# Loading the next image into a tile of its own during the last MLP, with its statistics taken there and its chunks copied on GpSimd

## The chip, the core and the metric

The kernel runs on one core of one Trainium2 chip. The metric is the device time in microseconds (us) of one execution; lower is better. The engines of the core run side by side, each with its own queue in order: TensorE (PE, with its weight loads as PEld), VectorE (DVE), ScalarE (ACT), GpSimd (POOL), and SyncE (SP), which here only issues DMAs.

## The reference, cut to what matters

Four images of 56 x 56 pixels and 128 channels pass through four layers. Each layer reads the group norm of its input and adds its result to it. Layers 0 and 3 are the same block with other weights.

```python
def _gn(v, G=32, eps=1e-5):
    B_, H_, W_, C_ = v.shape
    g = v.reshape(B_, H_, W_, G, C_ // G)
    m = jnp.mean(g, axis=(1, 2, 4), keepdims=True)
    s = jnp.var(g, axis=(1, 2, 4), keepdims=True)
    return ((g - m) / jnp.sqrt(s + eps)).reshape(v.shape)

x = x + L0(_gn(x), ...)   # window attention, full attention, MLP
x = x + L1(_gn(x), ...)   # 3x3 convolution, four selective scans (mamba)
x = x + L2(_gn(x), ...)   # deformable convolution
x = x + L3(_gn(x), ...)   # as L0
```

The blocks L0 and L3 ("swin" in the kernel) compute, for an image x:

```python
xs = roll(x, (-3, -3)); wins = 7 x 7 windows of xs
x = roll(windows_back(mha(wins)), (3, 3))
xf = x + mha(layernorm(x))             # attention over all 3136 pixels
xf = xf + gelu(layernorm(xf) @ w1 + b1) @ w2 + b2
```

The statistics of the group norm are over a whole image, so no part of a layer can start before the last pixel of its input is there.

## The kernel before, in words

An image lies on chip as one tile `x` of 128 channels (partitions) by 3136 pixels, float32. `x` is allocated once and holds every image in turn and every layer's result. All layers cut the 3136 columns into seven chunks of 448 (`NCK` chunks of `CH`).

`run` (L1415) loads image 0 into `x` and then, for each of the four images, takes the seven statistics (`stats`, L115: one `bn_stats` on VectorE for each chunk, into the small tile `gn_st`) and calls the layers L0, mamba, deform and L3. Inside a layer the statistics for the next layer are taken as each chunk is stored, so that the loop of `stats` in `run` is needed only where an image comes in.

A swin block is `attention` and then `mlp`. `attention` begins with `group_norm` (L123): the seven statistics are aggregated (L128, VectorE), two products of one column on TensorE average over groups (L130, L137), ScalarE takes a square root (L139) and VectorE its reciprocal (L140). Then come the windows, eight bands of them, in the order 3, 4, 5, 6, 7, 0, 1, 2. `tokens` (L230) zeroes the padded tiles of a band on GpSimd for the first two bands (memsets at L232 and L238; further ones for `ks`, `qs` and `kl` at L336, L337 and L391) and writes the normalized pixels of the band (L235: on VectorE for the first two bands, on GpSimd for the others). The full attention follows. It takes nearly all of a block's time.

`mlp` (L653) works through the chunks in the order 3, 4, 5, 6, 0, 1, 2 (`cols`). For each chunk `residual` adds the attention's result (L667, L668), `center`, `spread`, `scale` and `shift` are the layer norm (L154, L674 on GpSimd, L180, L679, L683, L687), `hidden` and `result` are the two products with the gelu between (L694, L695, L701), and `store` adds the chunk's result and writes it to `x` (L705, VectorE). The order in each queue is written out by hand: the loop at its end calls these steps for different chunks in turn, and a scheduler keeps that order within the block.

After a store, the L0 MLP takes the chunk's statistics. The L3 MLP (`last` is the number of the image there) calls `finish` instead: a DMA on SP writes the chunk to the output, and if there is a next image, a second DMA on SP loads the next image's chunk into the same columns of `x`. It waits until the first has landed. The seven statistics of the new image are issued by `run`, and stand among the MLP's instructions on VectorE as its scheduler placed them.

Of the kernel before, what the change touches and what calls it, by code (L numbers as in the profile page):

```python
# [10 lines left out]
F32 = mybir.dt.float32  # L11
# [8 lines left out]
P = 128  # L20
HW = 56
L = HW * HW
CH = 448
NCK = L // CH
# [54 lines left out]
class _Net:  # L79
# [573 lines left out]
    def mlp(self, layer, x, x1, oT, last):  # L653


        nc, tc, w = self.nc, self.tc, self.w[layer]
        with tc.tile_pool(name="mlp", bufs=2) as sb, tc.tile_pool(name="mlp_ps", bufs=8, space=PSUM) as ps, tc.manual_schedule():
            bank = lambda name: ps.tile([P, 512], F32, tag="mm", name=name)
            x2, m = x1, {}

            def cols(n):
                c = (n + 3) % NCK
                return slice(c * CH, (c + 1) * CH)

            def residual(n):
                py = bank("py2")
                nc.tensor.matmul(py[:, :CH], lhsT=w["wo"], rhs=oT[:, n * CH : (n + 1) * CH], start=True, stop=True)  # L667
                nc.vector.scalar_tensor_tensor(x2[:, cols(n)], py[:, :CH], w["boe"], x1[:, cols(n)], ALU.add, ALU.add)  # L668

            def center(n):  # L670
                (m["pc", n],) = self.ln_center([x2[:, cols(n)]], bank)
                m["sq", n] = sb.tile([P, 2, CH], F32, tag="ln_sq", name="ln_sq")
                nc.scalar.activation(m["sq", n][:, 0, :], m["pc", n][:, :CH], AF.Square)
                nc.gpsimd.tensor_add(x2[:, cols(n)], x2[:, cols(n)], x[:, cols(n)])  # L674

            def spread(n):
                sq = m["sq", n]
                self.ln_root(sq[:, 1, :], sq[:, 0, :], bank)
                nc.vector.reciprocal(sq[:, 1, :], sq[:, 1, :])  # L679

            def scale(n):
                sq = m["sq", n]
                nc.vector.tensor_mul(sq[:, 0, :], m.pop(("pc", n))[:, :CH], sq[:, 1, :])  # L683

            def shift(n):
                m["xn", n] = sb.tile([P, CH], F32, tag="xn2", name="xn2")
                nc.scalar.activation(m["xn", n], m.pop(("sq", n))[:, 0, :], AF.Identity, bias=w["be2"], scale=w["g2"])  # L687

            def hidden(n, fs):
                for f in fs:  # L690
                    if f == 0:
                        m["h", n] = sb.tile([P, 4, CH], F32, tag="h", name="h")
                    ph = bank("ph")
                    nc.tensor.matmul(ph[:, :CH], lhsT=w["w1"][:, f * P : (f + 1) * P], rhs=m["xn", n], start=True, stop=True)  # L694
                    nc.scalar.activation(m["h", n][:, f, :], ph[:, :CH], AF.Gelu, bias=w["b1"][:, f : f + 1])  # L695

            def result(n):
                h = m.pop(("h", n))
                py = bank("py3")
                for f in range(4):  # L700
                    nc.tensor.matmul(py[:, :CH], lhsT=w["w2"][:, f * P : (f + 1) * P], rhs=h[:, f, :], start=(f == 0), stop=(f == 3))  # L701
                m["py", n] = py

            def store(n):
                nc.vector.scalar_tensor_tensor(x[:, cols(n)], m.pop(("py", n))[:, :CH], w["b2"], x2[:, cols(n)], ALU.add, ALU.add)  # L705
                if last is not None:
                    self.finish(last, x, cols(n))
                else:
                    self.stats(x, (n + 3) % NCK)

            def do(f, n, *args):
                if 0 <= n < NCK:
                    f(n, *args)

            residual(0)
            residual(1)
            center(0)
            residual(2)
            spread(0)
            for n in range(-1, NCK):  # L720
                do(hidden, n, (0, 1))
                do(scale, n + 1)
                do(center, n + 2)
                do(hidden, n, (2, 3))
                do(shift, n + 1)
                do(residual, n + 4)
                do(spread, n + 2)
                do(result, n)
                do(store, n)


    def mamba_prepare(self):
# [673 lines left out]
                    product(NCK - 1, i)  # L1406
                add(NCK - 1)

    def finish(self, b, x, cols):

        self.nc.sync.dma_start(self.out[b][:, cols], x[:, cols])
        if b + 1 < self.B:
            self.nc.sync.dma_start(x[:, cols], self.x_in[b + 1][:, cols])

    def run(self):  # L1415
        x = self.x
        self.nc.sync.dma_start(x, self.x_in[0])
        self.swin_prepare("L0")
        self.swin_prepare("L3")
        self.mamba_prepare()  # L1420
        self.deform_prepare()
        for b in range(self.B):
            for c in range(NCK):
                self.stats(x, c)
            self.swin("L0", x)
            self.mamba(b, x)
            self.deform(b, x)
            self.swin("L3", x, last=b)
# [89 lines left out]
```

## Time and profile before

| what | us |
|---|---|
| time, median of 3 runs | 13293.08 (13291.37 to 13294.18) |
| profiled execution, its own time | 13095.61 |
| profiled execution, span from first to last instruction | 13093.7 |
| PE busy | 11654.7 (89% of the span) |
| VectorE busy | 9728.0 (74%) |
| ScalarE busy | 7560.0 (58%) |
| GpSimd busy | 9942.8 (76%) |
| mean granted TensorE clock | 0.943 of full speed |

The profiled execution is one run of its own, and 1.5% shorter than the median of the timed ones. One image takes about 3270 us of the span: the last stores of images 0, 1 and 2 start at 3276.30, 6546.27 and 9812.85 us. Busy shares are averages over stages with different limits; what happens between two images is seen only in the timeline at those places. In a line of the timeline the first number is the start in us from the start of the span, the second the duration in us, then come the engine, the line of the kernel, the operation, the tile written and the tiles read, the shapes, and the count of instructions merged into the line. A bracket gives the engine's idle time ahead of the line and what ended it. Of several instructions merged, the duration is that of all.

### The profile page before, as it was taken

To read this page: it belongs to the slowest core of one execution; us is meant where nothing else is said; L and a number is where in the kernel's file an instruction comes from. 1 tells how busy PE (TensorE), PEld (TensorE's weight loads), DVE (VectorE), ACT (ScalarE), POOL (GpSimd) and SP (SyncE) were. 2 spreads that over 40 slices of the span, in tenths; PEclk is the share of its full clock that TensorE was granted. 3 is DMA by queue.
4 is the path that set the end of the run, shared out by engine and by line. 5 is a ranking of instruction groups with operands and counts; after the bars stand their busy time and mean duration, and the time that the engine had idled before them with its cause. 6 is when DMAs were issued, how large, how long until landed. Compare 5 with 4: busy or idle time off the path is not lost. (4 is left out here: it accounts for less than half of the span.)

```text
span 13093.7 us, 216642 instructions
## 1 busy us (share of the span) xinstructions
PE 11654.7 (89%) x84932; PEld 7362.6 (56%) x84932; DVE 9728.0 (74%) x11883; ACT 7560.0 (58%) x19097; POOL 9942.8 (76%) x6852
## 2 busy tenths in 40 slices
PE   8989996799898999679989899967999989996799
PEld 4438884444543888444454388844445438884444
DVE  6659996665665999666566599966656659996665
ACT  5567772356556777235655677723565567772356
POOL 4949995498494999549759499954974949995497
PEclk9999997899999999789999999978999999997899
DMA  1000003200000000420000000042000000004200
GB/s 59 1 14 4 5 4 114 74 1 9 3 1 14 4 5 4 116 72 1 10 2 1 14 5 5 4 120 68 1 11 1 1 14 5 5 4 121 66 1 6
DMA packets 155644, 317.88 MB, mean 24 GB/s; under 512 B 19660, under 2 KB 89344, under 8 KB 154496
## 3 DMA queue, kind: packets, MB, share of 16 engines
q0 software_dynamic: 80640, 231.28, 6.1%
q1 hardware_dynamic: 73696, 71.21, 1.8%
q8 instruction: 672, 11.01, 0.3%
q14 instruction: 348, 2.85, 0.1%
q10 hardware_dynamic: 288, 1.53, 0.0%
HBM read 256.04 MB, written 47.90 MB: 23 GB/s over the span
## 5 line engine op out<-in xcount | busy, mean ns | idle before, releaser
L569 POOL TENSOR_TENSOR es<-es,e 128x896 f32<-128x896 f32 x2016 | 4159.3, 2090 | 133.1 <-ACT e L563 75.1
L363 DVE TENSOR_REDUCE mx<-pm 128x1 f32<-128x512 f32 (+1 forms) x4928 | 3057.9, 671 | 1401.5 <-PE pm L362 787.3
L563 ACT ACTIVATE e<-pst 128x448 f32<-128x448 f32 (+1 forms) x5600 | 2678.4, 544 | 1886.8 <-PE pst L561 1351.4
L1083 DVE TENSOR_TENSOR_SCAN hs<-da,dbu 128x928 f32<-128x928 f32 x1792 | 3633.1, 2070 | 52.2 <-ACT dbu L1076 30.0
L1092 POOL TENSOR_TENSOR hs<-hs,cb 128x896 f32<-128x896 f32 x1792 | 3473.8, 1951 | 25.0 <-ACT carry L1087 20.3
L362 PE MATMUL pm<-ks,qs 32*128 32x512 f32 (+1 forms) x9856 | 2906.1, 633 | 13.3 <-DVE nm L384 7.8
L561 PE MATMUL pst<-qs,ks 32*128 32x448 f32 x11200 | 2684.0, 547 | 0.0
L1101 PE MATMUL yt<-w_C,hs 128*116 128x128 f32 x14336 | 1865.1, 273 | 1.1 <-POOL hs L1092 1.1
L556 PE MATMUL pst<-nm,sel 32*128 32x448 f32 x5600 | 1637.1, 614 | 0.0
L1101 PEld LDWEIGHTS yt<-w_C,hs 128*116 128x116 f32 x14336 | 1571.2, 135 | 2.1 <-POOL hs L1092 2.1
L1065 PE MATMUL dbu<-dgb,ut 112*128 112x224 f32 x7168 | 1258.6, 298 | 268.0 <-DVE hs L1083 267.8
L585 PE MATMUL po<-e,va 128*32 128x448 f32 (+1 forms) x11200 | 1350.8, 551 | 0.0
L362 PEld LDWEIGHTS pm<-ks,qs 32*128 32x128 f32 x9856 | 923.4, 185 | 746.2 <-DVE mx L363 619.3
L1065 PEld LDWEIGHTS dbu<-dgb,ut 112*128 112x128 f32 x7168 | 946.2, 192 | 533.1 <-DVE hs L1083 523.3
L1265 POOL DMA_INDIRECT g<-tab,idx x1008 | 940.8, 933 | 393.6 <-issue 283.1
L1019 ACT ACTIVATE da<-dl,A 128x112 f32<-128x112 f32 x3584 | 1193.9, 382 | 0.1
L561 PEld LDWEIGHTS pst<-qs,ks 32*128 32x128 f32 x11200 | 1096.8, 185 | 100.9 <-issue 12.7
L556 PEld LDWEIGHTS pst<-nm,sel 32*128 32x128 f32 x5600 | 569.9, 184 | 739.9 <-DVE mx L363 387.1
L1379 PE MATMUL pvt<-w_C,g 112*128 112x112 f32 x2016 | 366.7, 338 | 623.4 <-issue 520.4
L1380 ACT COPY vt<-pvt 128x336 f32<-128x336 f32 x336 | 147.2, 438 | 1126.5 <-PE pvt L1379 1126.5
L288 POOL TENSOR_TENSOR pz<-s,m 64x784 f32<-64x784 f32 x128 | 191.8, 1498 | 751.9 <-DVE m L285 520.0
L1087 ACT COPY carry<-hs 128x32 f32<-128x32 f32 x1792 | 397.2, 222 | 624.0 <-DVE hs L1083 615.9
(237 smaller groups left out, 15945.1 us busy)
## 6 DMA issues: line engine op xcount, KB each, us to landing
g<-tab,idx POOLq DMA_INDIRECT x1008, 3.4
tab<-zero SPq DMA_DIRECT2D x4, 3364.0 KB
dl_d<-dl SPq DMA_DIRECT2D x28, 448.0 KB
dl<-dl_d SPq DMA_DIRECT2D x56, 224.0 KB
tab<-gt SPq DMA_DIRECT2D x16, 448.0 KB
out_dram<-x SPq DMA_DIRECT2D x28, 224.0 KB
tab<-gt SPq DMA_DIRECT2D x16, 336.0 KB
x<-in_x_dram SPq DMA_DIRECT2D x21, 224.0 KB
```

The costliest lines, as they stand in the source:

```text
L362: nc.tensor.matmul(pm[:, :m], lhsT=qs[head(h), q.start : q.start + P], rhs=ks[head(h), keys], start=True, stop=True)
L363: nc.vector.tensor_reduce(mx[:, home[i][1], h, kc : kc + 1], pm[:, :m], AX.X, ALU.max)
L556: nc.tensor.matmul(t[:, :CH], lhsT=self.sel[head(h), :], rhs=nm[head(h), part(qc)], start=True, stop=False)
L561: nc.tensor.matmul(t[:, :CH], lhsT=ks[head(h), k * KB : (k + 1) * KB], rhs=qs[head(h), part(qc)], start=False, stop=True)
L563: nc.scalar.activation(e[:nk, j, :], t[:nk, :CH], AF.Exp, scale=SCALE)
L569: nc.gpsimd.tensor_tensor(s, es[g - 1, p][:nk] if k == 1 else s, e[:nk], ALU.add)
L585: nc.tensor.matmul(m["po"][head(h), :CH], lhsT=va[:nk, k, head(h)], rhs=src(h)[:nk], start=(k == 0), stop=(k == NKB - 1))
L1019: nc.scalar.activation(m["da"][:, :, n, 2:], dl(), AF.Exp, scale=A[:, j, n : n + 1])
L1065: nc.tensor.matmul(pu[:, 8 * h : 8 * h + 8, 2 + tb * TB : 2 + (tb + 1) * TB], lhsT=made[g]["ut", 2 * r + tb][:, d, :], rhs=made["r", g // ...
L1083: nc.vector.tensor_tensor_scan(flat(pairs[u // 2][:, d % 2]), flat(made[g]["da"][:, r]), flat(banks.pop(u)), 0.0, ALU.mult, ALU.add)
L1092: nc.gpsimd.tensor_tensor(hs, hs, made["r", g // 2]["cb"][:, :, r * HW : (r + 1) * HW], ALU.mult)
L1101: nc.tensor.matmul(sums[q][:YR, e * P : (e + 1) * P], lhsT=hs[:, n, :], rhs=self.ident, start=(n == 0), stop=(n == NST // 2 - 1), is_trans ...
```

## The change

In the L3 MLP of every image but the last, a tile `ahead` of a whole image is allocated, and one DMA on SP loads the next image into it at the start of the MLP. After each store the chunk's output DMA is issued as before, and then the statistics of one chunk of `ahead` are taken. One step later in the loop, GpSimd copies that chunk from `ahead` to `x` (`replace`), which has to wait until the output DMA has read the old chunk; the last copy stands behind the loop. `finish` goes, and `run` takes the statistics only for the first image.

```diff
             x2, m = x1, {}
 
+            ahead = None
+            if last is not None and last + 1 < self.B:
+                ahead = sb.tile([P, L], F32, tag="ahead", name="ahead", bufs=1)
+                nc.sync.dma_start(ahead, self.x_in[last + 1])
+
...
             def store(n):
                 nc.vector.scalar_tensor_tensor(x[:, cols(n)], m.pop(("py", n))[:, :CH], w["b2"], x2[:, cols(n)], ALU.add, ALU.add)
                 if last is not None:
-                    self.finish(last, x, cols(n))
-                else:
-                    self.stats(x, (n + 3) % NCK)
+                    nc.sync.dma_start(self.out[last][:, cols(n)], x[:, cols(n)])
+                if last is None or ahead is not None:
+                    self.stats(x if last is None else ahead, (n + 3) % NCK)
+
+            def replace(n):
+                if ahead is not None:
+                    nc.gpsimd.tensor_copy(x[:, cols(n)], ahead[:, cols(n)])
...
                 do(result, n)
                 do(store, n)
+                do(replace, n - 1)
+            replace(NCK - 1)
...
-    def finish(self, b, x, cols):
-
-        self.nc.sync.dma_start(self.out[b][:, cols], x[:, cols])
-        if b + 1 < self.B:
-            self.nc.sync.dma_start(x[:, cols], self.x_in[b + 1][:, cols])
-
...
         for b in range(self.B):
-            for c in range(NCK):
+            for c in range(NCK if b == 0 else 0):
                 self.stats(x, c)
```

## The prediction

> **What bounds the kernel now.** I read the page first. PE is busy for 89% of the span, and PE has the largest share of the chain that ended last; nothing in the page names the step from one image to the next. So I went to the step itself, at 3276 us (image 0 to 1), in the timelines of VectorE (DVE) and GpSimd (POOL). Columns: start, duration, engine, line, what, and in brackets the idle time before and what ended it.
>
> ```profile
> 3275.45 0.63 DVE L117 BATCH_NORM_STATS2 gn_st<-x 128x6 f32<-128x448 f32 x1 [3.19 <-DMA x<-in_x_dram]
> 3276.30 0.68 DVE L705 SCALAR_TENSOR_TENSOR x<-py,w_L,x 128x448 f32<-128x448 f32 x1 [0.23 <-PE py L701]
> 3281.52 0.63 DVE L117 BATCH_NORM_STATS2 gn_st<-x 128x6 f32<-128x448 f32 x1 [4.54 <-DMA x<-in_x_dram]
> 3282.18 0.34 DVE L128 BATCH_NORM_AGGREGATE gn_mv<-gn_st 128x2 f32<-128x42 f32 x1
> ...
> 3286.25 0.16 DVE L140 RECIPROCAL gn_rstd<-gn_rstd 128x1 f32<-128x1 f32 x1 [2.31 <-ACT gn_rstd L139]
> 3286.53 0.89 DVE L235 TENSOR_SCALAR xw<-x,gn_mean,gn_rstd 128x343 f32<-128x343 f32 x3
> ```
>
> The last store of the image starts at 3276.30. Its chunk goes out (issued 3277.01), the next image's chunk is loaded over it (issued 3278.99, when the output has landed), and only then do the last statistics run, at 3281.52. From the last store to the aggregate it is 5.88 us here, 5.80 at the second step (6546.27 to 6552.07) and 5.84 at the third (9812.85 to 9818.69): a wait for DMA on an idle machine. The chain of work that ended last, in order of time, agrees for the third step:
>
> ```profile
> 9815.53 2.48 DMA x<-in_x_dram
> ```
>
> So the transfer is on the path, three times per run, for under 6 us each.
>
> The same piece of code without a load exists in this trace, where the L0 MLP is followed by the mamba stage:
>
> ```profile
> 859.80 0.68 DVE L705 SCALAR_TENSOR_TENSOR x<-py,w_L,x 128x448 f32<-128x448 f32 x1 [4.67 <-PE py L701]
> 860.52 0.63 DVE L117 BATCH_NORM_STATS2 gn_st<-x 128x6 f32<-128x448 f32 x1
> 861.25 0.34 DVE L128 BATCH_NORM_AGGREGATE gn_mv<-gn_st 128x2 f32<-128x42 f32 x1
> ...
> 864.85 0.16 DVE L140 RECIPROCAL gn_rstd<-gn_rstd 128x1 f32<-128x1 f32 x1 [2.11 <-ACT gn_rstd L139]
> ```
>
> Here the aggregate follows the last store by 1.45 us, and the reciprocal follows the aggregate by 3.60 us; at the image step that is 4.07.
>
> What GpSimd does meanwhile matters for the change. At each image step it zeroes the tiles of the next attention in one train of eleven memsets, 3276.26 to 3285.21, and the first normalization (L235 on VectorE) starts at 3286.53, after the train. At the other attention, L3, no load is waited for and the two meet. In image 3:
>
> ```profile
> 12242.82 1.81 POOL L238 MEMSET pz<- 128x2048 f32 x1
> 12244.57 0.53 POOL L232 MEMSET xw<- 128x512 f32 x1
> 12245.03 0.74 POOL L238 MEMSET qp<- 128x768 f32 x1
> 12245.72 1.41 POOL L238 MEMSET kb<- 128x1568 f32 x1
> 12247.06 1.81 POOL L238 MEMSET pz<- 128x2048 f32 x1
> ```
> ```profile
> 12243.86 5.63 DVE L235 TENSOR_SCALAR xw<-x,gn_mean,gn_rstd 128x343 f32<-128x343 f32 x3
> ```
>
> Three instructions that take 0.89 us take 5.63, and end just behind the last memset (12248.87). In images 0, 1 and 2 (2437.20, 5707.60, 8973.90) the same three take 1.46, 1.10 and 1.36: they waited for the memset that was running and got in before the next. So VectorE was let in 3 times of 4, once at the same offset within the train as the time it was not.
>
> [...] here, issued by SP, the output takes 1.98 us from its issue to the issue that waits for it. [...] the trace of before has no GpSimd copy. [...] granted clock 1.00 up to 3280 us, 0.50 from 3281 to 3290.
>
> **The change, part by part** (image step at 3276; times of before unless "new").
>
> Load: 21 loads of 224 KB become 3 of 1568 KB, one at the start of each last MLP but the final one. SP has nothing else queued there. The tile takes over memory of the attention, which ends between 3208 (last scores) and 3215 (last GpSimd multiply L611, 3213.79 to 3214.93). The first image's load, of the same size, was issued at 2.12 and read at 16.01, with the weights in the same queues: 13.9 us at most. New landing 3229 at the latest; the first reader follows the first store at 3234.26. Slack over 5 us, cost nothing. If that cover were gone, VectorE would stand at its head with the MLP's next scale (L683) behind it, and the delay would count nearly in full.
>
> Statistics: 21 in number before and after. Now each stands behind its store and ahead of the next L683. The L0 MLP has just that order, and runs from its first L668 to its last store in 62.74 us (797.06 to 859.80); the L3 MLP before also takes 62.74 (3213.56 to 3276.30). PE is the bound there, and the 0.55 us hide. Nothing.
>
> SP: the waits of the loads on the outputs vanish; they held only SP.
>
> Copies on GpSimd: 21 new ones. Bounds for one: a memset of 512 takes 0.52, the two-input L674 of the same shape 1.13[...]. I take 0.6. Copies 0 to 4 fall in gaps of 6 to 8 us between L674s; copy 5 waits for its output (issued 3271.00) and is done by 3274. None of these is on a path: their cover is GpSimd's 16.13 us of idle time before the memsets. Copy 6 waits for the last output: 3279.0, ends 3279.6. The memsets are queued behind it on GpSimd, since their tiles reuse the MLP's memory; their train moves from 3276.26 to 3279.55, +3.3 us.
>
> Path: new aggregate 3276.30 + 1.45 = 3277.75 (gain 4.43). New reciprocal +3.60 = 3281.35: the PE's two tiny products now come before the clock drops, 0.47 gained. L235 is ready 0.28 later, at 3281.63, against 3286.53: **4.90 us earlier**, if nothing is in its way. But the train of memsets is: "kb" runs from 3279.55+1.57 = 3281.12 to 3282.52. If VectorE gets in behind it, L235 starts at 3282.52, and the gain is **4.0 us**. If it does not, it waits for the train's end, 3279.55+8.95 = 3288.50, and the step is 2.0 us *longer* than before. Copy 6 may also hold L134/L135 ([...]new 3278.83 to 3279.24) for up to 0.6; the wait for "kb" absorbs that. With a copy of 1.13 the train starts at 3280.1, L235 meets "qp" and starts at 3281.7 (gain 4.8), or at 3289.0 (loss 2.5). Later users of the zeroed tiles have room: the second tokens' tile is zeroed by new 3284.7 and wanted near 3288.
>
> Nothing else moves: first image, other stages and the final tail (no load there) are as before. Sum: 3 x 4.0 = 12.0 us. The profiled execution took 13095.61 us (span 13093.7); it would take 13083.6. The median of the runs shown is 13293.08, 1.5% more than the profiled execution, and I take the gain over unscaled, since it is made of DMA and VectorE time: **13281**.
>
> **Rivals.**
> 1. *The lock is lost at every step* (ends slower). Place: L235 against the memset train on GpSimd, which copy 6 has pushed into its way. Price: 2.0 to 2.5 lost at each step instead of 4.0 gained: +6 to +7.5, 13299 to 13301. It decides if VectorE loses at more than two steps of three. For it: image 3 of L3. Against: 3 of 4 meetings went the other way. Chance 0.08.
> 2. *Mixed*: one or two steps lost, gain 6.0 or 0: 13287 to 13293. Chance 0.33.
> 3. *No meeting*: the memsets are issued ahead of copy 6, or miss L235: up to 3 x 4.9 = 14.7, 13278. Chance 0.08.
> 4. *The load comes late*, so that the tile does not do what it is for: some 5 us of VectorE standing per step, +3 to +15 in the sum. Against: the slack above. Chance 0.03.
> Forecast 0.45; 0.03 for something I don't see.
>
> **How the numbers follow.** One measurement of this kernel can tell about 0.2%, 26.6 us, from no change. Every case above is inside that. Range: rival 3 less the 2.8 us spread of the runs shown and some margin, 13273, to nearly all steps lost, 13298; that leaves out rivals 1, 4 and the unseen, 0.14. Faster by over 0.2% would need twice what the wait holds: 0.03. Slower 0.03. Within 0.94.
>
> **What would show it.** Right: L117 in the L3 MLPs with no DMA wait; L128 1.45 us behind the last L705; the "ks" memset 3 us later, behind a copy; L235 stretched to near 1.5 us (won) or over 6 us (lost). Wrong: an L117 waiting for the load, an L705 that comes later than before, copies longer than 1.2 us, or a gain beyond 4.9 us at a step.

## The result, and the profile after

| | before, us | changed, us | ratio (95% interval) |
|---|---|---|---|
| timed together, medians of 13 runs each | 13296.54 | 13290.79 (13278.94 to 13302.19) | 0.9995 (0.9987 to 1.0003) |
| timed again later (18 and 13 runs) | 13110.45 | 13101.2 | 0.9992 (0.9984 to 1.0) |

No difference that a measurement of this kernel can tell. The forecast was 13281, range 13273 to 13298; the median lies 10 us above the forecast.

The profiled execution of the changed kernel took 13278.94 us (span 13277.0), against 13095.61 of before. The two spans must not be subtracted. From L2's `gn_rstd` to L3's of the same image, through the deform stage, in which nothing was changed, it is 395 to 399 us in this trace, 351 in that of before, and 351 to 354 in a second trace of the changed kernel; over four images that is 180 of the 183 us by which the two spans differ. So everything below is measured inside the image step, from the start S of the last store.

The timeline of VectorE and GpSimd of the changed kernel at the first image step (start, duration, engine, line, what; in brackets the idle time before and what ended it):

```profile
3330.34 0.68 DVE L710 SCALAR_TENSOR_TENSOR x<-py,w_L,x 128x448 f32<-128x448 f32 x1 [4.79 <-PE py L706]
3330.95 0.62 DVE L117 BATCH_NORM_STATS2 gn_st<-ahead 128x6 f32<-128x448 f32 x1
3331.60 0.34 DVE L128 BATCH_NORM_AGGREGATE gn_mv<-gn_st 128x2 f32<-128x42 f32 x1
...
3333.07 0.56 POOL L718 COPY x<-ahead 128x448 f32<-128x448 f32 x1 [5.44 <-DMA out_dram<-x]
...
3334.59 0.74 POOL L238 MEMSET qp<- 128x768 f32 x1
...
3335.26 0.16 DVE L140 RECIPROCAL gn_rstd<-gn_rstd 128x1 f32<-128x1 f32 x1 [2.11 <-ACT gn_rstd L139]
3335.27 1.41 POOL L238 MEMSET kb<- 128x1568 f32 x1
3335.53 3.10 DVE L235 TENSOR_SCALAR xw<-x,gn_mean,gn_rstd 128x343 f32<-128x343 f32 x3
3336.61 1.97 POOL L238 MEMSET pz<- 128x2048 f32 x1
3338.53 0.57 POOL L232 MEMSET xw<- 128x512 f32 x1
```

The wait for the load is gone: L117 follows the store, L128 stands 1.26 us behind it (before 5.88), the reciprocal 4.92 (9.95). But the copy has pushed the memsets, and L235, which took 0.89 us behind the finished train, takes 3.10 in the middle of it. The groups of that stretch, shapes kept apart (busy us, mean ns, idle before):

```profile
L235 DVE TENSOR_SCALAR xw<-x,gn_mean,gn_rstd 128x28 f32<-128x28 f32 x1 | 1.8, 1807 | 0.0
L235 DVE TENSOR_SCALAR xw<-x,gn_mean,gn_rstd 128x21 f32<-128x21 f32 x1 | 1.6, 1626 | 0.0
L235 DVE TENSOR_SCALAR xw<-x,gn_mean,gn_rstd 128x343 f32<-128x343 f32 x1 | 1.4, 1354 | 0.1
```

(The recorded durations of queued pieces overlap, so they add to more than 3.10.) A piece of 28 elements per partition took longer (1.81 us) than one of 343 (1.35). The first piece waited for "kb" and was let in: it ended at 3336.88, 0.20 behind the end of "kb" (3336.68). Then "pz" got in, and the small pieces waited for the whole of it: they ended at 3338.61 and 3338.63, "pz" at 3338.58; "pz" is itself 1.97 long instead of 1.81. In the chain of work that ended last, at the third step, L235 now stands where the transfer of 2.48 us stood before:

```profile
9971.30 0.17 DVE gn_rstd L140
...
9971.92 2.81 DVE xw L235 x3
9974.73 0.14 issue
9974.86 1.64 PE pq L243 x2
```

The rest is as it was: from its first L673 (before's L668) to its last store the MLP takes 62.74 us, before and after, with PE busy for 58.96 of it both times; its load is issued at 3262.40 and first read at 3288.80, without a wait.

The three steps, us behind the start of the last store (step 1, 2, 3):

| | before | changed | changed, second trace |
|---|---|---|---|
| reciprocal L140 | 9.95, 9.87, 9.91 | 4.92, 4.91, 4.92 | 4.92, 4.91, 4.92 |
| end of the three L235 | 11.12, 11.03, 11.43 | 8.29, 8.28, 8.33 | 8.29, 8.29, 8.32 |
| first softmax reciprocal L285 | 22.85, 22.75, 23.16 | 20.04, 21.82, 21.81 | 21.79, 21.82, 21.85 |

So 5 us are won at L140, 2.8 are left behind L235, and at most steps 1 is left at the first softmax. The second loss is TensorE's clock. Busy time of each engine by stretch of the changed kernel's trace, in the order PE, PE's weight loads, VectorE, ScalarE, GpSimd (with the count of instructions), then the granted clock, the DMA share and GB/s; first the first step, then the second:

```profile
3334.80:3338.20 3.40, 0.00 (x0) 0.00 (x0) 2.83 (x4) 3.33 (x6) 3.40 (x3) 0.50 0.00 0
3338.20:3341.60 3.40, 2.81 (x5) 1.56 (x6) 0.43 (x2) 0.80 (x3) 3.40 (x5) 0.50 0.00 0
3341.70:3345.00 3.30, 1.58 (x13) 1.42 (x12) 1.81 (x4) 3.05 (x7) 3.30 (x4) 1.00 0.01 2
```

```profile
6656.00:6659.30 3.30, 2.30 (x4) 1.38 (x5) 0.84 (x2) 1.02 (x4) 3.30 (x5) 0.50 0.00 0
6659.40:6662.70 3.30, 2.39 (x10) 1.81 (x10) 1.01 (x3) 2.65 (x7) 2.62 (x2) 0.50 0.00 0
6662.80:6666.10 3.30, 3.30 (x11) 3.30 (x12) 1.13 (x3) 1.36 (x2) 1.44 (x3) 0.50 0.00 0
6666.30:6669.00 2.70, 2.70 (x16) 2.13 (x15) 1.55 (x3) 0.52 (x1) 0.00 (x0) 1.00 0.00 0
```

The clock falls to 0.50 some 4 us behind S and comes back 6.83 us later at step 1, 13.65 at step 2, and 10.24 in the kernel before: two, four and three times 3.41. At step 1 the first stretch of that length with work on PE is 83% busy (2.81 of 3.40), and the clock is back at its end, 11.3 behind S. At step 2 the clock fell half a microsecond earlier (at S+4.0 instead of 4.45); the same work fills 70% of its stretch (2.30 of 3.30), the next holds a wait and fills 72% (2.39 of 3.30), the one after it is filled (3.30 of 3.30), and the clock is back only at 17.65. That the busy share of a stretch decides is the author's estimate from these stretches: no run varied it alone, and later in the trace a stretch of 3.41 us with PE busy throughout (from 3519.12) was followed by another at 0.50. The first products of the attention then run at half clock (0.50), and the first softmax comes 13.5 us behind L235's end instead of 11.75.

### The profile page after: what moved, and what is told of

It reads as the page before. It is cut to its first block, busy times and chain, and to the rows that moved or that the text cites. A ratio compares the mean times of both kernels' runs of the same rounds, so it can differ in the third digit from the quotient of the medians.

```text
span 13277.0 us, 216663 instructions
## 1 busy us (share of the span) xinstructions
PE 11557.6 (87%) x84932; PEld 7332.0 (55%) x84932; DVE 9744.4 (73%) x11883; ACT 7557.7 (57%) x19097; POOL 9960.9 (75%) x6873
## 4 chain that ended last, share of the span: by engine, by line
PE 61%; DVE 19%; another core or an unknown queue 6%; ACT 6%; issue 4%; POOL 3%; DMA 0%; SPq 0%; ACTq 0%; DVEq 0%; POOLq 0%
PE pm L362 13%; DVE hs L1094 12%; PE po L585 9%; PE pst L561 6%; PE pst L556 4%; PE yt L1112 4%; PE dbu L1076 4%; PE pyb L1128 2%; POOL hs L1103 2%; DVE mx L363 2%; DVE dgb L980 2%; PE pvt L1390 2%; PE pd L574 2%; PE pss L270 1%
## 5 line engine op out<-in xcount | busy, mean ns | idle before, releaser
L561 PEld LDWEIGHTS pst<-qs,ks 32*128 32x128 f32 x11200 | 1098.4, 185 | 102.1 <-issue 13.7
L1390 PE MATMUL pvt<-w_C,g 112*128 112x112 f32 x2016 | 333.4, 332 | 905.9 <-issue 563.5
L1390 PEld LDWEIGHTS pvt<-w_C,g 112*128 112x128 f32 x2016 | 283.9, 184 | 984.1 <-issue 646.9
```

The costliest lines, as they stand in the source:

```text
L561: nc.tensor.matmul(t[:, :CH], lhsT=ks[head(h), k * KB : (k + 1) * KB], rhs=qs[head(h), part(qc)], start=False, stop=True)
```

## The experiments

The theory: the 2.2 us by which L235 is stretched (3.10 instead of 0.89) are waits for memsets that GpSimd is running, met piece by piece and not once for the group, and where the copy has put the train of memsets decides what L235 meets. (The recorded texts call this wait the lock; the word stands for the measured wait and for nothing behind it.) The rival: L235 waits for data or for GpSimd's count, or the copy itself holds it. Two more questions: whether the long L3 starts come from the program (an L3 start is the three L235 at the beginning of L3's attention, "blocked" where they take over 5 us; "draw" is used for a meeting whose outcome is not foreseen), and where the rest of the step could go. e0, e1, e3, e7 and e10 are one run each, and 18 runs of the kernel before spread over 46 us (13088.27 to 13133.97), so these five are read by their traces and not by their times.

**e0_before_again: the kernel before once more.** No edit.

> The kernel before, unchanged, for a second trace of it beside the other runs. Nothing is removed. [...]at the three image steps the three L235 follow the train of memsets and take 0.9 us, ending 11.1 us behind the last store; at the four L3 starts each of them is a draw, 1.1 to 1.5 us (let in) or near 5.6 us (blocked to the train's end), and the pattern need not be that of the first trace (in, in, in, blocked). Rival, a fixed order of events: the same pattern as in the first trace, 1.46, 1.10, 1.36 and 5.63 us. Total: if the 198 us by which the profiled executions of before and of the changed kernel differ come from the execution, this one may lie anywhere from 13096 to 13300.

Measured: 13104.4 us. Image steps 11.03, 11.04 and 11.44, as before; L3 starts 1.23, 1.10, 1.36 and 1.25 us: none blocked. Not a fixed order of events.

**e1_one_port: L235 in another form.**

```diff
-                (nc.vector if t < 2 else nc.gpsimd).tensor_scalar(xv[:, a, r, c], self.piece(img, at), gn[0], gn[1], ALU.subtract, ALU.mult)
+                src = self.piece(img, at)
+                if t < 2:
+                    for k in range(a.stop - a.start):
+                        dst = xv[:, a.start + k, r, c]
+                        nc.vector.scalar_tensor_tensor(dst, src[:, k], gn[0], gn[1][:, :, None].to_broadcast(list(dst.shape)), ALU.subtract, ALU.mult)
+                else:
+                    nc.gpsimd.tensor_scalar(xv[:, a, r, c], src, gn[0], gn[1], ALU.subtract, ALU.mult)
```

> The changed kernel with L235 for the first two tokens made one scalar_tensor_tensor per window (9 instead of 3 instructions for the first token; the second operand is rstd spread over the window)[...]. The train of memsets stays where it is. Theory [...]: nine pieces of 0.12 to 0.17 us run beside the memsets, first start 5.2 us behind the last store, last end 6.4 to 6.8 us behind it, where the changed kernel has 8.3; and at all four L3 starts the group takes under 2 us, so about 5 us at the image steps and 4 to 13 us at L3 are saved in the whole run. Rival (L235 waits for data or for GpSimd's count[...]): the last end stays at 8.3 us or later, and one or more of the L3 starts still take over 5 us.

Measured: 13101.75 us (one run; before beside it 13107.7). Its timeline at the first step:

```profile
3292.41 0.56 POOL L724 COPY x<-ahead 128x448 f32<-128x448 f32 x1 [5.44 <-DMA out_dram<-x]
3292.47 0.51 DVE L135 SCALAR_TENSOR_TENSOR gn_dv<-gn_dv,gn_mv 128x1 f32<-128x1 f32 x1
...
3294.60 1.40 POOL L244 MEMSET kb<- 128x1568 f32 x1
3295.36 1.66 DVE L239 SCALAR_TENSOR_TENSOR xw<-x,gn_mean,gn_rstd 128x49 f32<-128x49 f32 x9
3295.95 1.80 POOL L244 MEMSET pz<- 128x2048 f32 x1
```

Nine instructions run in 1.66 us straight through the end of "kb" and the start of "pz", and neither memset is longer for it. They end 7.33, 6.85 and 6.84 us behind the store (8.3 in the changed kernel), with three times as many instructions, and the four L3 starts take 1.66 each. The rival falls. (This is called the `scalar_tensor_tensor` form below, and L235 as it was the `tensor_scalar` form; `one_port` in three labels is only a name for the former.) Why this form does not wait beside a memset was not shown. The edit changes the number of pieces too, but small pieces alone do not escape: those of 28 and 21 elements waited in the old form. (One group took 0.18 us each and not 0.12 to 0.17, and step 1 ended late, at 7.33, for another reason that the fence shows: L134 began 0.19 later behind the store than in the changed kernel, and L135, also a `scalar_tensor_tensor`, took 0.51 instead of 0.22 beside the copy and ended with it, at 3292.98 and 3292.97, and rstd came 0.5 later. So beside a copy that form did take longer, beside the memsets it did not.)

**e3_double_copy: more work on GpSimd ahead of the memsets.**

```diff
             replace(NCK - 1)
+            replace(NCK - 1)
```

> The changed kernel with the last copy of each image issued twice: 0.56 us more work on GpSimd ahead of the memsets, nothing else. Theory (lock, and where the train stands): the train starts 3.9 instead of 3.36 us behind the last store; L235, ready 5.2 us behind it, now meets the qp memset, is let in at its end near 5.9, so that the first piece ends near 6.3 and the rest meets kb, ending near 7.4 if it is let in behind kb: earlier than the 8.3 of the changed kernel, with more work in the program. It can also lose the draw and end at 12.8. Rival (the copy itself or GpSimd's order holds L235): 0.56 later, 8.9.

Measured: 13105.11 us. At the first step:

```profile
3288.62 1.19 POOL L718 COPY x<-ahead 128x448 f32<-128x448 f32 x2 [5.44 <-DMA out_dram<-x]
...
3290.76 0.74 POOL L238 MEMSET qp<- 128x768 f32 x1
3291.09 1.97 DVE L235 TENSOR_SCALAR xw<-x,gn_mean,gn_rstd 128x343 f32<-128x343 f32 x3
3291.44 1.57 POOL L238 MEMSET kb<- 128x1568 f32 x1
3292.95 1.85 POOL L238 MEMSET pz<- 128x2048 f32 x1
```

L235 starts 5.19 behind the store as in the changed kernel, now meets "qp"; its first piece is let in at the end of that, the small ones wait for "kb", and it ends at 7.16 at steps 1 and 2: 1.1 us *earlier* than in the changed kernel, for a copy more. At step 3 it took 3.42 and ended at 8.96: there "kb" kept its 1.41 and "pz" was stretched to 1.97, so VectorE was first let in behind "kb". The size was foreseen to 0.3 us at steps 1 and 2. Step 3 alone, which was not foreseen, has the rival's figure (8.9); it is the stretched memset there that speaks for the theory. The copy is not what holds L235; the memsets that it meets are.

**e7_in_place: the same end without copies.** From the kernel before; `more` is true in an L3 MLP with a next image, and `y` is `x2` in every L3 MLP and `x` in the L0 MLP; `run` takes the statistics only for the first image, as in the changed kernel.

```diff
             def center(n):
...
                 nc.gpsimd.tensor_add(x2[:, cols(n)], x2[:, cols(n)], x[:, cols(n)])
+                if more:
+                    nc.sync.dma_start(x[:, cols(n)], self.x_in[last + 1][:, cols(n)])
...
             def store(n):
-                nc.vector.scalar_tensor_tensor(x[:, cols(n)], m.pop(("py", n))[:, :CH], w["b2"], x2[:, cols(n)], ALU.add, ALU.add)
+                nc.vector.scalar_tensor_tensor(y[:, cols(n)], m.pop(("py", n))[:, :CH], w["b2"], x2[:, cols(n)], ALU.add, ALU.add)
                 if last is not None:
-                    self.finish(last, x, cols(n))
-                else:
+                    nc.sync.dma_start(self.out[last][:, cols(n)], y[:, cols(n)])
+                if last is None or more:
                     self.stats(x, (n + 3) % NCK)
```

> The kernel before with another way to the same end: in the last MLP the store writes its result to x2 and the output leaves from there, the next image's chunk is loaded straight into x behind the last reader of that chunk (the GpSimd add of the norm's input), and its statistics follow the store. No copy and no tile of its own. Theory (lock): the aggregate is 1.3 us behind the last store and L235 is ready at 5.2, as in the changed kernel, but the train of memsets starts at 0 again and L235 meets its second half (kb or pz of the second token, 5.3 to 8.9): the last end is anywhere from 6.3 (let in at once) to 9.8 (blocked to the end), gains of 1.3 to 4.8 us per step against before. Rival (the copies hold L235): without them L235 runs unstretched, 5.2 to 6.1, at all three steps.

Measured: 13111.18 us. At the first step:

```profile
3288.72 0.74 POOL L238 MEMSET qp<- 128x768 f32 x1
3288.82 2.20 DVE L235 TENSOR_SCALAR xw<-x,gn_mean,gn_rstd 128x343 f32<-128x343 f32 x3
3289.40 1.57 POOL L238 MEMSET kb<- 128x1568 f32 x1
3290.92 1.85 POOL L238 MEMSET pz<- 128x2048 f32 x1
```

The train is back at the store, L235 meets its second "qp" and ends at 7.39 at all three steps. It is stretched without any copy in the program. The first softmax is 3.6 to 4.0 us earlier at each step than before, some 11 in the sum, and yet the run was 3.5 us longer than the kernel before beside it, which is inside the spread of single runs; all four L3 starts were blocked in this execution (5.64, 5.64, 5.44 and 5.44 us).

**e9_after_again and e10_before_third: who sets the L3 starts.** No edits.

> The changed kernel, unchanged, for a second trace of it. Lock as a draw: the image steps as before (L235 ends near 8.3 us behind the last store), the four L3 starts each 1.1 to 1.5 or near 5.6 us, not the same pattern as in its first trace (blocked, blocked, blocked, in). Rival (something in the program sets it): again mostly blocked, as in the first trace, in e3 and in e7, and the change then costs some 12 to 17 us at the L3 starts. The first softmax comes 11.8 us behind the end of L235 at some steps and 13.5 at others[...]. Time against before: 0.9995 within 0.001.

> The kernel before, unchanged, for a third trace. Lock as a draw: at least one of the four L3 starts is blocked for over 5 us, as one was in the first trace and none in the second. Rival (something in the program sets it): none or one blocked again, where e3, e7 and the changed kernel had 11 of 12 blocked.

Measured: 13101.2 and 13121.07 us. First L3 start of each trace, the changed kernel and then the kernel before:

```profile
2441.86 1.81 POOL L238 MEMSET pz<- 128x2048 f32 x1
2442.89 1.46 DVE L235 TENSOR_SCALAR xw<-x,gn_mean,gn_rstd 128x343 f32<-128x343 f32 x3
2443.61 0.69 POOL L232 MEMSET xw<- 128x512 f32 x1
```

```profile
2443.76 1.81 POOL L238 MEMSET pz<- 128x2048 f32 x1
2445.00 5.43 DVE L235 TENSOR_SCALAR xw<-x,gn_mean,gn_rstd 128x343 f32<-128x343 f32 x3
2445.51 0.53 POOL L232 MEMSET xw<- 128x512 f32 x1
```

The changed kernel: 1.46, 1.10, 0.96, 1.46, none blocked (first trace 5.64, 5.29, 5.54, 1.46). The kernel before: 5.43, 1.58, 5.12, 5.64, three blocked (first traces one and none). Both programs have both outcomes (4 of 12 starts of the kernel before are blocked, 3 of 8 of the changed one), so blocked starts do not come with the change. Over the seven traces with the old form of L235 there, 15 of 28 starts were blocked (the expectation of e11 below says 14, one miscounted). Within a trace they mostly go the same way; why was not tried and stays open.

The same seven traces also correct the picture of a draw for each piece. L235 meets the train 40 times in them, 28 times at L3 and 12 at image steps, with two outcomes only. In 15 meetings, all at L3, the first piece waited to the end of the train. In the other 25 it was let in at the next end of a memset (twice, where it came 0.11 and 0.22 us before that end, at the one after), and in all 25 the small pieces then waited for exactly one whole memset more; the memset behind the first piece is 0.17 us longer, the one behind the small pieces 0.04. So "draw" is fit only for the choice between these two outcomes. At L3, L235 always met "pz"; at the image steps it met "kb" or "qp" and was never blocked. Whether that decides is open.

At the image steps the changed kernel's two traces agree to 0.05 us at L235, and the first softmax of the second trace came 13.5 behind it at all three steps.

**e11_one_port_timed (the kernel of e1) and e2_before_one_port (the same edit in the kernel before), timed.**

> The kernel of e1 once more, timed[...]. From the traces so far: the image steps save 3.7 to 4.5 us each against before (first softmax 18.6 to 19.1 behind the last store, before 22.8), 12 in all; the four L3 starts save the draws. In the seven traces[...], 14 of 28 starts took over 5 us, each some 4 longer than the others: 8 us in the mean per run, less 0.4 at each start let in. Theory (lock as a draw, no other cost): 17 to 20 us less than before, ratio 0.9985 to 0.9987. Rival (the rest of e6's gain comes from the early norm, and the lock draws hide behind other work): 5 to 12 us, 0.9991 to 0.9996.

> The kernel before with only L235 of the first two tokens[...]: the draws at the L3 starts without the change. Image steps 0.8 us longer each (nine instructions of 1.66 instead of 0.89, behind the train anyway), L3 starts always 1.66. Theory (lock as a draw): 8 us less at L3 in the mean, 2.4 more at the steps, up to 2 more at the first image: 4 to 6 us less, ratio 0.9995 to 0.9998. Rival (the draws hide behind other work): 2 to 5 us more, 1.0001 to 1.0004. The two differ by less than one measurement of this kernel can tell, so the trace decides: all four starts at 1.66 and the first softmax there 13.4 to 15.4 behind the reciprocal.

Measured, against 13105.75 of before: e11 13087.27, ratio 0.9986 (0.998 to 0.9993), as the theory had it, though the interval reaches into the rival's 0.9991 to 0.9996; its steps end at 7.34, 6.84 and 6.85. e2 13105.95, ratio 0.9997 (0.9989 to 1.0005), which cannot choose; its four L3 starts take 1.66 each, and its first softmax there comes 13.7 behind the reciprocal (15.3 at the first). At its image steps the first softmax came at 25.4, 25.3 and 25.5, 2.3 to 2.5 later than before for a normalization only 0.8 longer. It is the clock again: it was back 21.0, 21.0 and 21.5 us behind the store, and 14.5 to 14.6 in the kernel before. The stretches at the third step of e2, in the view used above:

```profile
9837.82:9841.22 3.40, 2.68 (x4) 1.51 (x5) 0.57 (x4) 2.36 (x5) 0.00 (x0) 0.50 0.00 0
9841.24:9844.64 3.40, 2.50 (x11) 2.18 (x10) 1.41 (x6) 2.94 (x7) 1.27 (x1) 0.50 0.00 0
9844.65:9848.05 3.40, 3.40 (x12) 3.40 (x11) 1.78 (x7) 1.07 (x1) 1.34 (x3) 0.50 0.00 0
9848.05:9851.40 3.35, 3.09 (x17) 2.33 (x16) 1.68 (x4) 1.20 (x3) 0.00 (x0) 1.00 0.00 0
```

So, by the traces, the `scalar_tensor_tensor` form pays where L235 meets the train, and it is the change that makes it meet the train at the image steps too.

**e6_early_norm: what is left of the step.** e7 with e1's L235, and the norm of the next image inside the last MLP; `norm_steps` holds the instructions of `group_norm`, parted by `yield`: the aggregate behind the sixth store; then, around the last chunk, the first product with mean and deviations, the second product, the root, and behind the store the reciprocal. The next attention takes this mean and rstd in place of its own `group_norm`.

```diff
             for n in range(-1, NCK):
                 do(hidden, n, (0, 1))
                 do(scale, n + 1)
                 do(center, n + 2)
+                if norm:
+                    next(norm)
                 do(hidden, n, (2, 3))
+                if norm:
+                    next(norm)
...
                 do(result, n)
+                if norm:
+                    next(norm)
                 do(store, n)
+                if norm:
+                    next(norm)
+                if more and n + 1 < NCK:
+                    self.stats(x, (n + 4) % NCK)
+                if more and n + 2 == NCK:
+                    norm = self.norm_steps(self.keep, bank)
+                    next(norm)
```

> A version for speed. As in e7 the load goes straight into x behind its last reader and the output leaves from x2; the statistics of chunk n+1 follow the store of chunk n, the aggregate the sixth store, and the two small products, the root and the reciprocal are put between the steps of the last chunk, so that mean and rstd are there at the last store[...]. Theory (what is left of the step is the chain of the statistics plus the lock): nothing of the norm is left behind the last store but the root; L235 starts when the first xw memset is done, 1.0 to 1.5 us behind the last store, ends at 2.7 to 3.2, and the first softmax reciprocal, 11.8 behind that, comes near 14.8 instead of 22.8: 8 us at each of three steps, 24 in all, and 0 to 17 more at the L3 starts by how many draws the kernel before loses, less 1 to 3 at the first image. 20 to 40 us, 0.15 to 0.3%. Rival (the last chunk's MLP pays for what is put into it): the small products wait on TensorE for VectorE and the last store comes 1 to 4 us later, so that 4 to 7 us per step are left, 10 to 20 in all.

Measured: 13068.37 us against 13110.45, ratio **0.9968 (0.9956 to 0.998)**. At the first step:

```profile
3276.01 0.34 DVE L148 BATCH_NORM_AGGREGATE ga_mv<-gn_st 128x2 f32<-128x42 f32 x1
...
3280.39 0.26 ACT L159 ACTIVATE ga_rstd<-ga_pv,eps 128x1 f32<-128x1 f32 x1
...
3282.10 0.69 DVE L738 SCALAR_TENSOR_TENSOR x<-py,w_L,x 128x448 f32<-128x448 f32 x1 [4.65 <-PE py L734]
3282.12 0.52 POOL L254 MEMSET xw<- 128x512 f32 x1
...
3282.70 0.15 DVE L161 RECIPROCAL ga_rstd<-ga_rstd 128x1 f32<-128x1 f32 x1
3282.96 1.66 DVE L261 SCALAR_TENSOR_TENSOR xw<-x,ga_mean,ga_rstd 128x49 f32<-128x49 f32 x9
```

The aggregate stands 6.1 us ahead of the last store, the root ahead of it too, and L235's successor ends at 2.52, 2.59 and 2.60. The first softmax comes at 13.98, 13.64 and 14.14: 8.9 to 9.1 us earlier than before at each step, 27.0 in all (8 and 24 were expected); e1 and e11, with the `scalar_tensor_tensor` form but the norm behind the store, gained 12.4 there. That leaves some 15 of the 42 us by which the medians differ; the L3 draws explain about 8 of those, by an estimate from the ends of L235 (15 of 28 blocked, 4 starts, 4.2 us each, less 0.4 for each let in), and the remainder is inside the interval (26 to 58 us at 13110).

## Why the prediction was right, and where it was not

*No change that can be measured*: right, and for the reason given: the wait for the load is the whole stake, under 6 us at three places. That the median fell into the range says nothing for the working below it: every case that was priced, won or lost, lay within 0.2%.

*Load, statistics, SP at no cost*: right. First read 26.4 us behind its issue; MLP 62.74 both times.

*Copies 0.6 each, copy 6 waiting for the last output, the train 3.3 later*: right. 0.56 each; copy 6 at S+2.73; "xw" at S+3.78 (before 0.38), so 3.4.

*Aggregate at S+1.45, reciprocal 3.60 behind it, L235 ready 4.90 earlier*: right to 0.2. S+1.26, 3.66 behind, 5.04 earlier at step 1.

*L235 waits for "kb", is let in behind it, gain 4.0 per step*: the wait for a memset was right, and so was the place, and this is the term that was mis-sized. The working let L235 start anew at the end of "kb" and then take its 0.89. At the first step VectorE was let in behind "kb", but for one piece only; the small pieces waited for the whole of "pz". The end came at S+8.29, where the working has 7.11 (start 3282.52, 0.89 long, S 3276.30); the other five recorded steps end within 0.04 us of it. L235's end gained 2.83, 2.75 and 3.10 us, 8.7 in all instead of 12.0. Rivals 1 and 2, in which the whole group is blocked to the train's end, did not occur at a step. With "pz" at its 1.97 in place of the 0.89, the same working gives an estimate of about 8.2. The L3 meetings that the working took for its model had the same wait. In image 0 of the kernel before:

```profile
2437.20 1.46 DVE L235 TENSOR_SCALAR xw<-x,gn_mean,gn_rstd 128x343 f32<-128x343 f32 x3
2437.91 0.69 POOL L232 MEMSET xw<- 128x512 f32 x1
```

The group ends at 2438.66, just behind "xw" at 2438.60, so only its first piece had got in before the next memset. A short memset stood behind "pz" there, and the wait hardly showed.

*"Nothing else moves"*: wrong by the clock. TensorE restarts about 8.45 us behind the store and not 11.2 to 11.6, and the return of the clock does not move with it: it came 11.28, 17.65 and 17.58 us behind the store in the first trace, and 14.54 to 14.56 before. At five of the six steps this cost 1.7 to 1.8 us, and of 8.7 us 5.1 arrived at the first softmax in the first trace (2.81, 0.93 and 1.35) and 3.3 in the second. Before, e1 and e7 keep 11.7 to 11.8 from L235's end to the first softmax at all their steps; in the trace of before PE is busy for 3.30, 3.39 and 2.96 of the 3.41 us that end with the clock's return.

*The sum*: 12.0 forecast, 3.3 to 5.1 in the traces, 5.75 and 9.25 between medians whose intervals are some 20 us wide. That the medians and the traces agree is likely, not shown: a run's L3 draws alone, estimated from the ends of L235, move it by up to 17 us.

## What to carry to other kernels

A stall that is removed hands over to what comes next in time: list what runs on the other engines at the next instruction's *new* start (here GpSimd's memsets, beside which the three L235 took 3.10 us and not 0.89), and do not cost a group of small instructions as one: here the rest of the group waited for one whole memset more in all 25 meetings in which its first piece was let in. An instruction form that does not wait can be worth more than an earlier start, even with three times the instructions (1.66 us beside the same memsets): at the three steps the earlier start gave 3 to 5 us, and 12 with that form. And where the whole stake is a chain of small dependent steps behind a barrier (statistics, aggregate, product, root), moving the whole chain ahead of the barrier as well gave 27 us.

## What was not expected of the hardware

- The same start had two outcomes: at the same offset in the train, to 0.01 us (3.53 us behind the start of its first "xw" memset), the three L235 took once 1.46 us in all and once 5.64, both in the first trace of the changed kernel. Who lost once was not ahead at the next: behind the memset that was running, four more went by in each of the 15 blocked meetings.
- The clock was back at 1.00 behind a stretch of 3.4 us in which PE was 83% busy (2.81 of 3.40); stretches of 70%, 72% and, in e2, 79% (2.68 of 3.40) were followed by more at 0.50. It stayed low for 6.83, 10.24 and 13.65 us, whole multiples of 3.41.
- A GpSimd copy of 448 float32 elements per partition, SBUF to SBUF, took 0.56 us, close to a memset of 512 (0.53).
